# A fused attention and gated MLP kernel: where the MLP output's row pairs, its last gates and its last two token tiles stand

## The chip, the core and the metric

The kernel runs on one core of one Trainium2 chip. The core has five engines that run side by side and meet through semaphores: TensorE (PE, matmuls, with its weight loads shown as PEld), VectorE (DVE), ScalarE (ACT), GpSimd (POOL) and SyncE (SP, which here issues the DMAs). The metric is the device time of one launch in microseconds, the median of a few runs. Lower is better.

## The reference

The input x has shape (2, 2048, 256). It is layer-normalised to xn, and two branches read xn: a global attention s with 16 heads, and a two-layer local network, whose SiLU gates s. Cut to what matters here:

```python
xn = layernorm(x)
s = attn_ref(xn)                   # 16 heads of 16, spatial bias, projection, + layernorm(xn)
h = xn
for l in range(2):                 # DEPTH
    h = h + local_attention(shift(h)) @ wo[l]          # 8 heads of 64, windows of 128
    a, g = split(layer_norm(shift(h)) @ w1[l] + b1[l]) # 682 columns each
    h = h + (a * gelu(g)) @ w2[l] + b2[l]
return x + s * silu(h)
```

All numbers are float32. shift moves the second half of the features by one token.

## The kernel before

The program first runs the global attention (to about 1690 us) and writes s to DRAM. The local network, `ffn_branch`, takes the rest. It works on **slots**: slot s is one layer, one batch and one chunk of 512 tokens, 16 slots in all, in the order layer, chunk, batch. Slots 0 to 7 belong to layer 0, 8 to 15 to layer 1. Each slot has four token tiles of 128. The loop (from `for n in range(len(tiles) + 4)`) runs one **step** per tile, n = 4 s + i, with i from 0 to 3, plus four steps after the last tile. The order of the work is written out by hand: `STEP` lists the operations of a step, and nothing is reordered later.

- T0, T1 (`a_turn`, L969): transposes of q and k of the tile before. Each is a set of matmuls that use half of the array's rows, in pairs for the rows 0 to 63 and 64 to 127. W0, W1 (`a_weights`, L1057) are half-row transposes as well, S0, S1 (`a_scores`, L997) use quarters, A0, A1 (`a_sums`, L1077) half of the columns. Everything else on PE uses the full array.
- R hands out the pieces of the layer norm's root (`f_var_at`), Q, K, V (`a_project`, L924) project the tile.
- F runs what is in `xs`: at i = 1 the attention's output for slot s-1 (`a_out`, L1092), at i = 2 and 3 the MLP's output for slot s-3, half k = 0 and 1 (`f_out`), and at i = 3 the mean for slot s-1 (`f_mean`, L1115).
- the three G take pieces from `gq`, the MLP's gates of slot s-2. A gate m has a matmul for its Gelu half (n = 1, then ScalarE, L1179) and one for its linear half (n = 0, then VectorE writes u, L1183). Per step i = 0, 1, 2, 3 they take 5, 2, 2 and 3 pieces.

The 682 hidden columns are five full blocks of 128 and a sixth of 42. `f_last` (L1195) computes the sixth with both halves in one matmul; VectorE writes `u_last` on 42 partitions (L1199) and POOL copies it to the partitions 64 and up (L1202). `u_last` is one buffer for all slots. In `f_out` the sixth block is a **row pair** (`both_halves`, L1214): two matmuls with 64 rows each, one in each half of the array, into two PSUM banks. float32 makes two passes of each, so the profile counts four.

In layer 0 `f_out` has 20 matmul passes into two banks `py`, the pair, and then two VectorE adds into the running state (`residual`, L902). The last token's column is held back in `held` until `f_mean` of the next chunk has read it. In layer 1 a half k is two token tiles: for each, ten passes into `pz` and two transposes of the state into `pzx` (L1242, L1248); then the pair, VectorE's `y = pzx + b2` (L1255) and two adds of `pz` (L1257). A closure `gate` is put into `gates`: SiLU on ScalarE, two POOL operations with s and x (L1261, L1262), and the store by SP. Gates run at the end of the step that made them. s and x of a half are loaded at the start of its first part, into one buffer each.

PSUM has eight banks, and `bank` hands them out in turn: a new tile waits for those that read the tile eight calls earlier. A DMA of `nc.sync` waits in SP's queue, in order.

After the loop, slots 14 and 15 are finished by hand: gates and outputs in turn, then all gates that are left.

Of the kernel before, what the change touches and what calls it, by code (L numbers as in the profile page):

```python
# [12 lines left out]
AF = mybir.ActivationFunctionType  # L13
ALU = mybir.AluOpType
# [3 lines left out]
B, N, D = 2, 2048, 256  # L18
P = 128
NT = N // P  # L20
CH = 512
NCH = N // CH
# [13 lines left out]
NM = (HID + P - 1) // P  # L36
MASKED = -1e30
HALVES = [slice(r * HD2, (r + 1) * HD2) for r in range(2)]
# [782 lines left out]
def ffn_branch(  # L821
# [9 lines left out]
    nc = tc.nc  # L831
    with ExitStack() as ctx:
# [3 lines left out]
        W, load_scales, load_tables, load_qkv, load_o, load_1, load_2 = weights  # L836
# [3 lines left out]
        h, mw = P // 2, HID - (NM - 1) * P  # L840
# [3 lines left out]
        u_last = cp.tile([P, CH], F32, name="u_last")  # L844
# [15 lines left out]
        def bank(name, shape=(P, CH)):  # L860
            turn[0] += 1
            return psr.tile(list(shape), F32, tag=BANKS[turn[0] % 8], name=name)
# [16 lines left out]
        def all_due():  # L879
            while later:  # L880
                later.pop(0)[1]()
# [6 lines left out]

        held = {}

        def residual(kind, b, cc, k, ps, col, part=slice(0, CH)):


            at = 1 + cc * CH + part.start
            w = part.stop - part.start
            n = w if k == 0 or cc == NCH - 1 or part.stop < CH else w - 1
            x = xA[b][:, k, at : at + w]
            if n < w:
                h = pool.tile([P, 1], F32, tag=f"held{kind}{b}", name=f"held{kind}_{b}_{cc}")
                nc.vector.scalar_tensor_tensor(h, ps[:, n:w], col, x[:, n:], ALU.add, ALU.add)  # L900
                held[kind, b] = (cc, h)
            nc.vector.scalar_tensor_tensor(x[:, :n], ps[:, :n], col, x[:, :n], ALU.add, ALU.add)  # L902

        def release(kind, b):
            if (kind, b) in held:
                cc, h = held.pop((kind, b))
                at = (cc + 1) * CH
                nc.vector.tensor_copy(xA[b][:, 1, at : at + 1], h)
# [202 lines left out]
        def f_mean(s):  # L1111
            l, b, cc = slots[s]
            hs = halves(s)
            pm = bank(f"pm_{s}")
            nc.tensor.matmul(pm, mean_w, fs[s]["hc"][:, 0, :], start=True, stop=True)  # L1115
            hc = fs[s]["hc"]
            for k in range(2):
                nc.vector.tensor_sub(hc[:, k, :], hs[k], pm)
            release("f", b)
            sq = pool.tile([P, 2, CH], F32, tag="sq", name=f"sq_{s}", bufs=1)  # L1120
            fs[s] = {"hc": hc, "sq": sq, "u": {}}
            soon(1, lambda: nc.scalar.activation(sq, hc, AF.Square))
            soon(2, lambda: nc.gpsimd.tensor_add(sq[:, 0, :], sq[:, 0, :], sq[:, 1, :]))
# [37 lines left out]
        def f_gate(s, m, n):  # L1161

            l, b, cc = slots[s]
            nm = f"{s}_{m}_{n}"
            V = vecs[:, l, :]
            mw = min(P, HID - m * P)
            at = n * HID + m * P
            if mw < P:
                return f_last(s, m, mw)
            hc = fs[s]["hc"]  # L1170
            assert fs[s].get("ready")
            ps = bank(f"pg_{nm}")
            for k in range(2):
                nc.tensor.matmul(  # L1174
                    ps[:mw], W["1"][:, k, at : at + mw], hc[:, k, :], start=(k == 0), stop=(k == 1)
                )
            if n == 1:
                gl = next_gl(nm)
                nc.scalar.activation(gl[:mw], ps[:mw], AF.Gelu, bias=V[:mw, NM + m : NM + m + 1])  # L1179
                fs[s]["gl"] = gl  # L1180
            else:
                u = pool.tile([P, CH], F32, tag="u", name=f"u_{nm}", bufs=8)
                nc.vector.scalar_tensor_tensor(  # L1183
                    u[:mw], ps[:mw], V[:mw, m : m + 1], fs[s]["gl"][:mw], ALU.add, ALU.mult
                )
                fs[s]["u"][m] = u

        def f_last(s, m, mw):
# [12 lines left out]
            )  # L1201
            soon(1, lambda: nc.gpsimd.tensor_copy(u_last[h : h + mw], u_last[:mw]))  # L1202

        def f_out(s, k, part):

            l, b, cc = slots[s]
            F = fs[s]
            V = vecs[:, l, :]
            full = NM - 1

            def both_halves(to, lhs, rhs):

                for q, rows in enumerate(HALVES):
                    nc.tensor.matmul(to[q], lhs(q)[rows], rhs(q)[rows], start=False, stop=True)  # L1214

            if l < DEPTH - 1:
                cols = [slice(q * CH // 2, (q + 1) * CH // 2) for q in range(2)]
                w2 = W["2"][:, :, k * P : (k + 1) * P]
                if part == 0:
                    F["py"] = [bank(f"py_{s}_{k}_{q}")[:, : CH // 2] for q in range(2)]  # L1220
                for q in range(2):
                    for m in range(3 * part, min(3 * part + 3, full)):
                        nc.tensor.matmul(
                            F["py"][q], w2[:, m, :], F["u"][m][:, cols[q]], start=(m == 0), stop=False
                        )
                if part == 1:
                    both_halves(F["py"], lambda q: w2[:, full, :], lambda q: u_last[:, cols[q]])
                    c0 = 2 * NM + 4 + k
                    for q in range(2):
                        residual("f", b, cc, k, F["py"][q], V[:, c0 : c0 + 1], cols[q])  # L1230
                return
            if part == 0:
                F["py"] = [bank(f"pz_{s}_{k}_{q}")[:, :D] for q in range(2)]
                F["xt"] = bank(f"pzx_{s}_{k}", (P, 2, D))
                F["s"] = shared(0, (P, 2, D), f"s_{s}_{k}")
                F["x"] = shared(1, (P, 2, D), f"x_{s}_{k}")
                F["y"] = shared(2 + k, (P, 2, D), f"y_{s}_{k}")
                nc.sync.dma_start(F["s"], s_out[b * NCH + cc][:, 2 * k : 2 * k + 2, :])
                nc.sync.dma_start(F["x"], x_ch[b * NCH + cc][:, 2 * k : 2 * k + 2, :])
            i = 2 * k + part  # L1240
            for m in range(full):
                nc.tensor.matmul(  # L1242
                    F["py"][part], F["u"][m][:, i * P : (i + 1) * P], W["2"][:, m, :], start=(m == 0),
                    stop=False,
                )
            for h in range(2):
                at = 1 + cc * CH + i * P
                nc.tensor.transpose(F["xt"][:, part, h * P : (h + 1) * P], xA[b][:, h, at : at + P], ident)  # L1248
            if part == 1:
                both_halves(  # L1250
                    F["py"], lambda q: u_last[:, (2 * k + q) * P : (2 * k + q + 1) * P],
                    lambda q: W["2"][:, full, :],
                )
                y, ys, yx = F["y"], F["s"], F["x"]
                nc.vector.tensor_add(y, F["xt"], b2_row[:, None, :].to_broadcast([P, 2, D]))  # L1255
                for q in range(2):
                    nc.vector.tensor_add(y[:, q, :], y[:, q, :], F["py"][q])  # L1257

                def gate():
                    nc.scalar.activation(y, y, AF.Silu)  # L1260
                    nc.gpsimd.tensor_mul(y, y, ys)  # L1261
                    nc.gpsimd.tensor_add(y, y, yx)  # L1262
                    nc.sync.dma_start(out_ch[b * NCH + cc][:, 2 * k : 2 * k + 2, :], y)

                gates.append(gate)


        gates = []
# [7 lines left out]
        def gate_pieces(s):  # L1276
            full = NM - 1
            ps = [(lambda m=m, n=n: f_gate(s, m, n)) for m in range(full) for n in (1, 0)]
            return ps[:4] + [lambda: f_gate(s, full, 1)] + ps[4:]

        clear(k_ring[0][:, :, P : 2 * P], *sms[:4])
        gq = []
# [1 line left out]
        for n in range(len(tiles) + 4):  # L1284
            s, i = divmod(n, TPC)
            cur, pre, pre2 = (tiles[x] if 0 <= x < len(tiles) else None for x in (n, n - 1, n - 2))
            order = START_STEPS[n] if n < 2 else FIRST_STEP if n <= N_FIRST else STEP

            def have(x):
# [35 lines left out]
            def run(q, n=1):  # L1325
                for _ in range(n):
                    if q:
                        piece(q.pop(0))
# [48 lines left out]
                load_o(1)  # L1377
            if s == per_layer + 2 and i == 0:
                load_1(1)
            if s == per_layer + 2 and i == 3:  # L1380
                load_2(1)
        s = n_slots + 1
        run(gq, 99)
        for k in range(2):
# [7 lines left out]
            g()  # L1392
        gates.clear()
        run(gq, 99)
        for k in range(2):
            run(out_pieces(s - 2, k), 2)
        all_due()
        for g in gates:
            g()
        gates.clear()  # L1400


# [87 lines left out]
```

## Time and profile before

| what | value |
|---|---|
| median of 3 runs | 3005.99 us (3005.26 to 3006.25) |
| the profiled execution's own time | 3006.25 us |
| its span, first to last instruction | 3004.5 us |
| mean granted TensorE clock | 0.995 |
| the stretch 1880 to 2500 us: PE, DVE, ACT, POOL busy | 620.0, 407.2, 374.7, 396.2 us |
| the stretch 2500 to 2910 us: PE, DVE, ACT, POOL busy | 410.0, 268.7, 266.8, 274.9 us |
| last store issued | 3001.15 us |

The span is what the hardware profiler sees from the first instruction to the last; the time of the same execution is a little longer. Busy times come from the stretches view. A timeline line gives the start in us, the length in us, the engine, the source line, the operation, its tiles (out<-in), shapes and the number of merged instructions; in brackets the idle time before it and what ended that. Lengths of matmuls are modelled and overlap the next one, so on PE the distance between starts is what counts. A waits view lists which engine waited for which, in total, how often and the longest.

### The profile page before, as it was taken

How to read it: one execution, taken by the hardware profiler on the slowest of the kernel's cores; microseconds unless marked ns; L12 is line 12 of the kernel's file. 1: busy time of each engine (PE TensorE's matmuls, PEld its weight loads, DVE VectorE, ACT ScalarE, POOL GpSimd, SP SyncE). 2: the span in 40 equal slices, each digit the busy share in tenths (PEclk: the TensorE clock that was granted, in tenths of full speed). 3: DMA queues.
4: the chain of work that ended last, by engine and by line, in shares of the span. 5: the costliest groups of instructions: out<-in, count | busy, mean ns of one | idle time of the engine just before them, and what ended most of it. 6: DMA issues, size and time to landing. Idle time of an engine off the chain costs nothing. (4 is left out here: it accounts for less than half of the span.)

```text
span 3004.5 us, 60909 instructions
## 1 busy us (share of the span) xinstructions
PE 2964.5 (99%) x22764; PEld 1368.1 (46%) x22764; DVE 2211.6 (74%) x4840; ACT 2125.3 (71%) x4528; POOL 1618.2 (54%) x1463
## 2 busy tenths in 40 slices
PE   8999999999999999999999999999999999999998
PEld 3433333333333333333333465555555555565565
DVE  6898888788887788888885576666666666666653
ACT  4788877788887788888888655656666556666653
POOL 3575434446544354353444565666666666667642
PEclk9999999999999999999999999999999999999999
DMA  3100100000001100010000200000000000000001
GB/s 122 31 8 17 35 18 25 30 15 21 23 16 53 53 8 25 13 26 9 8 9 25 76 10 1 8 1 8 1 5 33 1 21 18 22 22 22 22 22 56
DMA packets 65963, 70.77 MB, mean 24 GB/s; under 512 B 28772, under 2 KB 44300, under 8 KB 65668
## 3 DMA queue, kind: packets, MB, share of 16 engines
q1 hardware_dynamic: 64770, 66.09, 7.3%
q8 instruction: 180, 2.95, 0.4%
q14 instruction: 115, 0.94, 0.1%
q10 hardware_dynamic: 386, 0.52, 0.1%
q0 software_dynamic: 512, 0.26, 0.0%
HBM read 45.35 MB, written 17.53 MB: 21 GB/s over the span
## 5 line engine op out<-in xcount | busy, mean ns | idle before, releaser
L439 DVE TENSOR_REDUCE mx<-pm 128x1 f32<-128x512 f32 x2048 | 1270.4, 683 | 218.3 <-PE ps L480 207.6
L482 ACT ACTIVATE e<-ps 128x512 f32<-128x512 f32 x2048 | 1058.3, 603 | 246.9 <-PE ps L480 245.6
L436 PE MATMUL pm<-kT,qT 32*128 32x512 f32 x4096 | 1020.1, 617 | 5.3 <-DVE mx L439 5.1
L480 PE MATMUL ps<-qa,kT 32*128 32x512 f32 x4096 | 1013.5, 616 | 0.0
L513 POOL TENSOR_TENSOR o<-o,part 128x512 f32<-128x512 f32 x465 | 590.0, 1269 | 776.5 <-ACT part L512 771.5
L436 PEld LDWEIGHTS pm<-kT,qT 32*128 32x128 f32 x4096 | 403.0, 184 | 409.9 <-DVE mx L439 385.2
L498 PE MATMUL po<-e,v 128*32 128x512 f32 x4096 | 546.6, 606 | 0.0
L480 PEld LDWEIGHTS ps<-qa,kT 32*128 32x128 f32 x4096 | 398.1, 184 | 187.2 <-ACT e L482 107.3
L1036 POOL TENSOR_TENSOR sm<-sm,wls 128x384 f32<-128x384 f32 x224 | 180.4, 826 | 339.5 <-DVE wls L1025 332.5
L924 PE MATMUL pp<-weights,xA 128*128 128x512 f32 x768 | 348.9, 601 | 0.0
L512 ACT COPY part<-po 128x512 f32<-128x512 f32 x465 | 287.0, 617 | 6.7 <-PE po L498 5.5
L1174 PE MATMUL pg<-hc,weights 128*128 128x512 f32 x640 | 286.2, 595 | 0.0
L498 PEld LDWEIGHTS po<-e,v 128*32 128x32 f32 x4096 | 81.0, 108 | 389.3 <-ACT e L482 359.7
L1019 ACT ACTIVATE sm<-sm,wmx 128x192 f32<-128x192 f32 x512 | 225.3, 441 | 8.9 <-DVE wmx L1011 8.2
L955 POOL TENSOR_TENSOR rn<-rn,mhalf 128x8 f32<-128x8 f32 x128 | 215.6, 1684 | 9.8 <-DVE rn L954 5.2
L924 PEld LDWEIGHTS pp<-weights,xA 128*128 128x128 f32 x768 | 141.6, 190 | 165.7 <-issue 164.4
L945 ACT ACTIVATE sqq<-pp 128x512 f32<-128x512 f32 x128 | 76.4, 597 | 173.9 <-DVE swp L943 157.6
L1174 PEld LDWEIGHTS pg<-hc,weights 128*128 128x128 f32 x640 | 120.5, 190 | 150.9 <-issue 143.3
L946 POOL TENSOR_TENSOR rot<-rot,swp 128x512 f32<-128x512 f32 x128 | 163.8, 1293 | 34.0 <-DVE swp L943 30.4
L1179 ACT ACTIVATE gl<-pg,vecs 128x512 f32<-128x512 f32 x80 | 54.6, 683 | 148.3 <-PE pg L1174 148.0
L1183 DVE SCALAR_TENSOR_TENSOR u<-pg,vecs,gl 128x512 f32<-128x512 f32 x80 | 59.8, 747 | 132.0 <-PE pg L1174 132.0
L1011 DVE CUSTOM_DVE_ANT_0 sm<-ps,mask 128x192 f32<-128x192 f32 x512 | 147.0, 354 | 4.7 <-PE ps L997 4.3
(183 smaller groups left out, 3415.3 us busy)
## 6 DMA issues: line engine op xcount, KB each, us to landing
s<-in_x_dram SPq DMA_DIRECT2D x8, 512.0 KB
qk_wk<-stage_wk SPq DMA_DIRECT2D x16, 256.0 KB
kT<-qk_wk SPq DMA_DIRECT2D x128, 32.0 KB
qk_wq<-stage_wq SPq DMA_DIRECT2D x16, 256.0 KB
qT<-qk_wq SPq DMA_DIRECT2D x128, 32.0 KB
qa<-qk_wq SPq DMA_DIRECT2D x128, 32.0 KB
s_out<-s SPq DMA_DIRECT2D x8, 512.0 KB
s<-s_out SPq DMA_DIRECT2D x16, 256.0 KB
```

Source lines behind the costliest of these rows:

```text
L436: nc.tensor.matmul(ps, qT[rows, q0 : q0 + P], kT[rows, c * CH : (c + 1) * CH], start=True, stop=True)
L439: nc.vector.tensor_reduce(mxs[n][:, j * TPC + i, c : c + 1], ps, AX.X, ALU.max)
L480: nc.tensor.matmul(ps, kT[rows, kt * P : (kt + 1) * P], qas[n % 2][rows, :], start=True, stop=True)
L482: nc.scalar.activation(e, ps, AF.Exp)
L498: nc.tensor.matmul(po[j * HP : (j + 1) * HP, :], v[:, kt, (r + j) * VW : (r + j) * VW + HP], es.pop((n, kt, j)), start=True, stop=True,)
L512: nc.scalar.copy(part, po)
L513: nc.gpsimd.tensor_add(os[n], os[n], part)
L924: nc.tensor.matmul(ps, xA[b][:, k, at : at + P], W["qkv"][:, k, n * INNER : (n + 1) * INNER], start=(k == 0), stop=(k == 1),)
L955: nc.gpsimd.tensor_tensor(rn, rn, mhalf, ALU.pow)
L1019: nc.scalar.activation(sm[:, x, IN], sm[:, x, IN], AF.Exp, scale=-1.0, bias=mx[:, hb, r, x : x + 1], accum_out=ls[:, hb, r, x : x + 1],)
L1036: nc.gpsimd.tensor_mul(sm, sm, ls[:, hb, r, :, None].to_broadcast([P, 2, WIN]))
L1174: nc.tensor.matmul(ps[:mw], W["1"][:, k, at : at + mw], hc[:, k, :], start=(k == 0), stop=(k == 1))
```

## The change

- In `f_out`, the pair and what reads it become a closure. For slots 0 to 12 it goes into `pairs`, and `close_pairs` runs it at the start of the next step, in front of that step's T0. For later slots it runs at once.
- Layer 0's adds (`rest`) stand behind the pair. Since they now come after `f_mean`, nothing is held back, and `release("f", b)` goes.
- In layer 1, `rest` also loads s and x (`load_sx`), and the gate it makes runs at the end of the step in which the pair stands.
- `f_last` moves from the fifth place of a slot's gate pieces to the ninth. So the step i = 3 ends with the Gelu half of gate 3, and `f_last` is in i = 0.
- Layer 1's w2 is loaded behind the first `close_pairs` of the next step.
- The last slot's half k = 1 is done tile by tile: transposes first, b2 added at once, the sixth block as one half-row matmul; SiLU on ScalarE, product and sum with s and x on VectorE, and a store for each tile. Its s and x have buffers of their own, loaded in its first part. The gate of k = 0 runs ahead of it.

The diff's core:

```diff
-            release("f", b)
+        pairs = []
+        def row_pair(s, to, lhs, rhs, then):
+            def f():
+                for q, rows in enumerate(HALVES):
+                    nc.tensor.matmul(to[q], lhs[q][rows], rhs[q][rows], start=False, stop=True)
+                then()
+            if s + 3 < n_slots:
+                pairs.append(f)
+            else:
+                f()
+        def close_pairs():
+            while pairs:
+                pairs.pop(0)()
+        def load_sx(s, k, tag):
...
+            for i, src in enumerate((s_out, x_ch)):
+                x = shared(tag + i, (P, 2, D), f"{'sx'[i]}_{s}_{k}")
+                nc.sync.dma_start(x, src[b * NCH + cc][:, 2 * k : 2 * k + 2, :])
...
+                def rest():
...
+                    for q in range(2):
+                        nc.vector.scalar_tensor_tensor(
+                            x[:, cols[q]], py[q], V[:, c0 : c0 + 1], x[:, cols[q]], ALU.add, ALU.add
                         )
                 if part == 1:
-                    both_halves(F["py"], lambda q: w2[:, full, :], lambda q: u_last[:, cols[q]])
...
+                    row_pair(s, py, [w2[:, full, :]] * 2, [u_last[:, c] for c in cols], rest)
                 return
+            last = s == n_slots - 1 and k == 1
             if part == 0:
...
-                nc.sync.dma_start(F["s"], s_out[b * NCH + cc][:, 2 * k : 2 * k + 2, :])
-                nc.sync.dma_start(F["x"], x_ch[b * NCH + cc][:, 2 * k : 2 * k + 2, :])
+                if last:
+                    F["sx"] = load_sx(s, k, 4)
...
+            if last:
+                turn_x()
+                nc.vector.tensor_add(y[:, part, :], xt[:, part, :], b2_row)
+            for m in range(full + last):
+                rows = HALVES[0] if m == full else slice(0, P)
+                u = (u_last if m == full else F["u"][m])[rows, i * P : (i + 1) * P]
+                nc.tensor.matmul(py[part], u, W["2"][rows, m, :], start=(m == 0), stop=last and m == full)
+            if last:
+                yp = y[:, part, :]
+                nc.vector.tensor_add(yp, yp, py[part])
+                nc.scalar.activation(yp, yp, AF.Silu)
+                nc.vector.tensor_mul(yp, yp, F["sx"][0][:, part, :])
+                nc.vector.tensor_add(yp, yp, F["sx"][1][:, part, :])
+                nc.sync.dma_start(out_ch[b * NCH + cc][:, i, :], yp)
+                return
+            turn_x()
+            def rest():
+                ys, yx = load_sx(s, k, 0)
+                nc.vector.tensor_add(y, xt, b2_row[:, None, :].to_broadcast([P, 2, D]))
...
+            if part == 1:
+                lhs = [u_last[:, (2 * k + q) * P : (2 * k + q + 1) * P] for q in range(2)]
+                row_pair(s, py, lhs, [W["2"][:, full, :]] * 2, rest)
...
-            return ps[:4] + [lambda: f_gate(s, full, 1)] + ps[4:]
+            return ps[:8] + [lambda: f_gate(s, full, 1)] + ps[8:]
...
+            close_pairs()
+            if s == per_layer + 3 and i == 0:
+                load_2(1)
...
-            if s == per_layer + 2 and i == 3:
-                load_2(1)
...
+        all_due()
         for k in range(2):
             run(out_pieces(s - 2, k), 2)
-        all_due()
-        for g in gates:
-            g()
-        gates.clear()
+            for g in gates:
+                g()
+            gates.clear()
```

More of the change, by code (lines that the diff above doesn't have):

```diff
@@ L889, in ffn_branch, with residual @@
         held = {}
[L891 to L898, printed above, removed]
+        def residual(kind, b, cc, k, ps, col):
+            at = 1 + cc * CH
+            n = CH if k == 0 or cc == NCH - 1 else CH - 1
+            x = xA[b][:, k, at : at + CH]
+            if n < CH:
                 h = pool.tile([P, 1], F32, tag=f"held{kind}{b}", name=f"held{kind}_{b}_{cc}")
-                nc.vector.scalar_tensor_tensor(h, ps[:, n:w], col, x[:, n:], ALU.add, ALU.add)
+                nc.vector.scalar_tensor_tensor(h, ps[:, n:], col, x[:, n:], ALU.add, ALU.add)
                 held[kind, b] = (cc, h)
@@ L1202, in f_last @@
             soon(1, lambda: nc.gpsimd.tensor_copy(u_last[h : h + mw], u_last[:mw]))
+        pairs = []
[12 more added lines that the diff above has]
+        def load_sx(s, k, tag):
+            l, b, cc = slots[s]
+            both = []
+            for i, src in enumerate((s_out, x_ch)):
+                x = shared(tag + i, (P, 2, D), f"{'sx'[i]}_{s}_{k}")
+                nc.sync.dma_start(x, src[b * NCH + cc][:, 2 * k : 2 * k + 2, :])
+                both.append(x)
+            return both
         def f_out(s, k, part):
@@ L1209, in f_out @@
             full = NM - 1
-            def both_halves(to, lhs, rhs):
-                for q, rows in enumerate(HALVES):
-                    nc.tensor.matmul(to[q], lhs(q)[rows], rhs(q)[rows], start=False, stop=True)
             if l < DEPTH - 1:
@@ L1220, in f_out @@
                     F["py"] = [bank(f"py_{s}_{k}_{q}")[:, : CH // 2] for q in range(2)]
+                py = F["py"]
                 for q in range(2):
                     for m in range(3 * part, min(3 * part + 3, full)):
-                        nc.tensor.matmul(
-                            F["py"][q], w2[:, m, :], F["u"][m][:, cols[q]], start=(m == 0), stop=False
+                        nc.tensor.matmul(py[q], w2[:, m, :], F["u"][m][:, cols[q]], start=(m == 0), stop=False)
+                def rest():
+                    c0 = 2 * NM + 4 + k
+                    x = xA[b][:, k, 1 + cc * CH : 1 + (cc + 1) * CH]
+                    for q in range(2):
+                        nc.vector.scalar_tensor_tensor(
+                            x[:, cols[q]], py[q], V[:, c0 : c0 + 1], x[:, cols[q]], ALU.add, ALU.add
                         )
                 if part == 1:
-                    both_halves(F["py"], lambda q: w2[:, full, :], lambda q: u_last[:, cols[q]])
-                    c0 = 2 * NM + 4 + k
-                    for q in range(2):
-                        residual("f", b, cc, k, F["py"][q], V[:, c0 : c0 + 1], cols[q])
+                    row_pair(s, py, [w2[:, full, :]] * 2, [u_last[:, c] for c in cols], rest)
                 return
+            last = s == n_slots - 1 and k == 1
             if part == 0:
@@ L1234, in f_out @@
                 F["xt"] = bank(f"pzx_{s}_{k}", (P, 2, D))
-                F["s"] = shared(0, (P, 2, D), f"s_{s}_{k}")
-                F["x"] = shared(1, (P, 2, D), f"x_{s}_{k}")
                 F["y"] = shared(2 + k, (P, 2, D), f"y_{s}_{k}")
-                nc.sync.dma_start(F["s"], s_out[b * NCH + cc][:, 2 * k : 2 * k + 2, :])
-                nc.sync.dma_start(F["x"], x_ch[b * NCH + cc][:, 2 * k : 2 * k + 2, :])
+                if last:
+                    F["sx"] = load_sx(s, k, 4)
             i = 2 * k + part
[L1241 to L1245, printed above, removed]
@@ L1246, in f_out @@
-            for h in range(2):
-                at = 1 + cc * CH + i * P
[L1248 to L1255, printed above, removed]
+            py, xt, y = F["py"], F["xt"], F["y"]
@@ new lines, in turn_x @@
+            def turn_x():
+                at = 1 + cc * CH + i * P
+                for h in range(2):
+                    nc.tensor.transpose(xt[:, part, h * P : (h + 1) * P], xA[b][:, h, at : at + P], ident)
+            if last:
[5 more added lines that the diff above has]
+                nc.tensor.matmul(py[part], u, W["2"][rows, m, :], start=(m == 0), stop=last and m == full)
@@ L1256, in f_out @@
                 for q in range(2):
-                    nc.vector.tensor_add(y[:, q, :], y[:, q, :], F["py"][q])
+                    nc.vector.tensor_add(y[:, q, :], y[:, q, :], py[q])
                 def gate():
```

## The prediction, made before the changed kernel was run

> **What bounds the kernel now.** I read the page first, then who waited for whom on PE, then the timeline of PE around one step's end, then VectorE's over the same microseconds, and last all engines in the tail.
>
> ```profile
> PE 2964.5 (99%) x22764; PEld 1368.1 (46%) x22764; DVE 2211.6 (74%) x4840; ACT 2125.3 (71%) x4528; POOL 1618.2 (54%) x1463
> ```
>
> PE is busy 99% of the span, and the list of waits on PE between 1900 and 2900 us has no line at all: from the first moved pair to the last, PE never waits and only streams. So time taken from PE's stream there is time gained, and any new wait of PE is time lost, one for one. PE's timeline (start, length, engine, line, operation) over a boundary of two steps in layer 0:
>
> ```profile
> 2398.19 0.71 PE L969 MATMUL pt<-ident,rot 64*128 64x64 f32 x16
> 2398.74 1.16 PE L1057 MATMUL pw<-ident,sm 64*128 64x64 f32 x32
> 2399.83 1.53 PE L997 MATMUL ps<-k_ring,xT 64*64 64x192 f32 x32
> ...
> 2408.45 4.48 PE L1223 MATMUL py<-u,w 128*128 128x256 f32 x20
> 2412.86 0.70 PE L1214 MATMUL py<-u_last,w 64*128 64x256 f32 x4
> 2413.49 1.13 PE L1115 MATMUL pm<-hc,mean_w 128*128 128x512 f32 x2
> 2414.45 1.88 PE L1195 MATMUL pg<-hc,weights 128*128 128x512 f32 x4
> ```
>
> The pair (L1214) stands between full-array matmuls and takes 2413.49 - 2412.86 = 0.63. Two other places show the same neighbours without the change of shape: a pair directly before half-row transposes, and pm (L1115) after a full-array matmul.
>
> ```profile
> 2917.51 0.70 PE L1214 MATMUL pz<-w,u_last 64*128 64x256 f32 x4
> 2918.04 1.16 PE L1057 MATMUL pw<-ident,sm 64*128 64x64 f32 x32
> ```
>
> ```profile
> 2938.30 1.02 PE L1115 MATMUL pm<-hc,mean_w 128*128 128x512 f32 x2
> 2939.16 3.60 PE L1174 MATMUL pg<-hc,weights 128*128 128x512 f32 x8
> ```
>
> **Part 1: what the move saves.** Before half-row transposes the pair takes 0.53 instead of 0.63. pm takes 0.86 instead of the 0.96 behind a pair: 0.10. The 20 py take 4.41 to the pair; the tail's ten L1242 take 2.16 (2993.52 to 2995.68), so 20 are 4.32 and entry costs 0.09. T0 and T1 (L969) take 0.55 from a full-array predecessor; half of L1057's 32 inside the mode, (1.09 - 0.09)/2, are 0.50: 0.05. T0's own entry is paid either way. Together 0.10 + 0.10 + 0.09 + 0.05 = **0.34 a pair**. Moved are slots 0 to 12, two pairs each: 26 x 0.34 = **8.8 us** off.
>
> **Part 2: the wait that takes its place.** Before, the pair's banks were read by VectorE under the gates' matmuls. Now the pair stands last, and the eight banks come round. Counting `bank` calls from the pair's first bank: in layer 0 after i=2 (py, py, two gates, T0 two, T1 two) W0 gets the pair's banks; after i=3 (py, py, pm, three gates, T0 two) T1 gets them. In layer 1 pzx takes one more: after i=2 T1's second and W0's first bank, after i=3 T0's second and T1's first. The built program has just these waits on VectorE's adds. VectorE at this boundary:
>
> ```profile
> 2394.66 0.88 DVE L902 SCALAR_TENSOR_TENSOR xA<-py,vecs,xA 128x256 f32<-128x256 f32 x2 [1.31 <-PE py L1214]
> ...
> 2398.37 0.75 DVE L1183 SCALAR_TENSOR_TENSOR u<-pg,vecs,gl 128x512 f32<-128x512 f32 x1 [2.83 <-PE pg L1174]
> 2399.04 0.75 DVE L978 COPY k_ring<-pt 128x256 f32<-128x256 f32 x2
> 2399.70 1.28 DVE L1060 COPY pT<-pw 128x512 f32<-128x512 f32 x2
> ```
>
> Set t=0 where T0 starts before (2398.19). The pair will start there, T0 at 0.53, T1 at 0.78, W0 at 1.03 if nothing waits. VectorE's first add can start 0.73 after the pair (2394.66 - 2393.93; the pair before it in the same timeline), and two take 0.88; PE follows VectorE by some 0.05 (k_ring's copies end at 2399.79, S0's matmuls start at 2399.83).
> - Layer 0, after i=2: the last gate's u (L1183) holds VectorE until 2399.04, t=0.85. Adds end at 1.73, W0's second bank comes at 1.78 instead of 1.03: **0.75**.
> - Layer 0, after i=3: the step now ends with a ScalarE gate, VectorE is free, adds run 0.73 to 1.61, T1's second bank comes at 1.66 instead of 0.78: **0.88**.
> - Layer 1, after i=2: b2's add (0.69) and two y adds, in the tail 2996.15 to 2997.70 = 1.55 (first y add done at 1.22), start at 0.85. T1 waits to 2.12, ends at 2.37, W0 waits for the second add, 2.40, to 2.45 instead of 1.03: **1.42**.
> - Layer 1, after i=3: b2's add needs no pair and is done early; the y adds run 0.73 to 1.48. T0's second bank comes at 1.20, T1's at 1.53, W0 at 1.78: 0.75. Then S0 (1.09 behind W0, 2.87) wants xT, and ScalarE has Gelu, Silu's table, Silu and the copies in a row:
>
> ```profile
> 2577.33 0.69 ACT L1179 ACTIVATE gl<-pg,vecs 128x512 f32<-128x512 f32 x1
> 2578.03 1.28 ACT L1260 ACT_TABLE_LOAD   x1
> 2579.32 0.63 ACT L1260 ACTIVATE y<-y 128x512 f32<-128x512 f32 x1
> 2579.86 0.63 ACT L973 COPY xT<-pt 128x256 f32<-128x256 f32 x2
> ```
>
> That is 3.16 from Gelu's start to both copies. Before, a second matmul gate (1.72) covered it; now Gelu is last and starts at about t=0.1 (0.20 behind its gate's matmuls, less T0's entry), so S0 waits to 3.32: 0.45 more, **1.20**.
>
> Stalls: 8 x (0.75 + 0.88) + 5 x (1.42 + 1.20) = 13.0 + 13.1 = **26.1**. Against 8.8 saved: **+17.3**. Bounds: by the nearest row of a pair without waiting, 0 (then -8.8 remains); above, 26 x 1.55 = 40 if the layer 1 chain were uncovered everywhere. I take the worked values, since each bank and its releaser is in the program and each length is a row.
>
> The Trainium skill has a rule on each side, on one page (TensorEngine Tiling): section Key Properties says that a change of tiling mode drains TensorE, section PSUM Bottleneck that tiling leaves PSUM evacuation as slow as it was. The 0.10 behind a pair is the first, the 0.88 of VectorE's adds the second; by the first alone the time would be 2997, by both it is the sum below.
>
> **Part 3: the smaller moves.** `u_last`'s STT (0.74) goes from i=3 into i=0, ahead of the fourth reciprocal, where VectorE idles 0.36 before the last u (2437.94): the k_ring copies there come some 0.1 to 0.25 later, and S0 (0.04 behind them at 2399.83) has nothing to spare. I take 0.1 in 14 steps: **+1.4** (0 to 3.5). In the first step after the last tile (2913.5) PE already waits 0.4 for a u that now stands behind `u_last`: **+0.6** (0 to 0.7). Costed at nothing: s and x loads and the gate a step later, on SP, ScalarE and POOL (PE's 18 to 21 us step covers them; transfers take 3.1, and SP's stores only queue behind that POOL work); the dropped `held` copies (VectorE idle 1.31 to 2.35 there); w2's load (two steps before use; the uncovered price would be one transfer). The i=3 to i=0 gate of ScalarE is counted above.
>
> **Part 4: the tail.** The last instructions before:
>
> ```profile
> 2995.58 1.27 POOL L1262 TENSOR_TENSOR y<-y,x 128x512 f32<-128x512 f32 x1
> ...
> 2996.15 0.69 DVE L1255 TENSOR_TENSOR y<-pzx,b_row 128x512 f32<-128x512 f32 x1 [4.04 <-POOL y L1261]
> 2996.88 0.37 SPq L1239 DMA_DIRECT2D x<-in_x_dram  x1
> 2996.95 0.75 DVE L1257 TENSOR_TENSOR y<-y,pz 128x256 f32<-128x256 f32 x2
> 2997.30 4.22 SPq L1263 DMA_DIRECT2D out_dram<-y  x2
> ...
> 2999.86 1.26 POOL L1262 TENSOR_TENSOR y<-y,x 128x512 f32<-128x512 f32 x1
> ```
>
> The last store is issued at 3001.15. Single tiles gated by VectorE would cut the chain, but `load_sx` for k=1 now comes in SP's order behind the store of k=0, which waits for POOL until 2996.85. So s and x are issued at about 2997.5 and 2997.9; issue to use took 3.1 for such an x (2977.42 to POOL's 2980.55), so the first tile's last add runs at 3001.0. Behind it on VectorE stands all of the second tile: that add, b2, py, product and sum at 0.42 each (a 256-wide L1257), Silu about 0.40 (between the 0.37 of a 256-wide copy and 0.63 for 512), gaps 0.3: 2.8, store at 3003.8: **+2.7**. With the loads early it would be -1.8: py of the last tile ends 0.8 later (its half-row matmul no longer shares a pass), then 0.42 + 0.40 + 2 x 0.42 and gaps put the store at 2999.4. I take +2.7 and keep both ends.
> The skill (DMA: Bandwidth & Descriptors, section Anatomy of one DMA) gives a fixed 2.0 us and 436 GB/s, by estimate 2.6 for 256 KB: the tail would be +2.2.
>
> **Sum.** 17.3 + 1.4 + 0.6 + 2.7 = +22.0. The profiled execution took 3006.25 (its span 3004.5 and 1.75 around it), 0.26 above the median 3005.99; from the median: **3028.0**.
>
> **Rivals.**
> - The switches alone (faster): at every moved pair VectorE's adds end before PE comes to the pair's banks, so only the 0.34 is felt: 3006.0 - 8.8 + 2.7 = 2999.9, or 2995.4 with early loads in the tail. For it, the switches are plain in PE's rows; against it, the adds' 0.88. It decides where 0.73 and the adds together stay under the 1.03 to W0 (layer 0, i=2), 0.30 for the two adds. 0.08.
> - The change half does what it says: the stalls are half covered, because T0 and T1 run on while VectorE ends: -8.8 + 13.0 + 4.7 = +8.9, 3015 and down to 3009 with the tail early. For it, VectorE's 0.85 at t=0 is one row's; against it, all boundaries of before look alike. 0.08, half of it counted within 0.2%.
> - Later engines do not catch up (exps and k_ring late as well, another 0.4 a boundary): 3036 to 3042. For it, VectorE runs without a gap from u through the sm rows; against it, the stall gives VectorE time. 0.05.
> - My sum: 0.79, of its own 3017 to 3036.
>
> **How the numbers follow.** 0.2% is 6 us, about what can be told from no change here. Faster by more: 0.08; within (3000 to 3012): 0.04; slower: 0.88. The range 3011 to 3037 holds the own range and part of two rivals, some 0.84, and the bounds of the tail (-4.5) and u_last (+2).
>
> **What would show it.** In the profile after: L1208's pairs right before L968 at 0.53; waits of PE pt and pw on DVE xA and y, 26 places, together near 25 us; pm back at 0.86; S0's wait on ACT xT five times; s and x of the last tiles issued after the store of k=0. Wrong if PE has no wait on those adds, or if its waits there stay under 10 us in all.

## The result, and the profile after

The changed kernel takes **3030.71 us** (median of 5 runs, 3029.75 to 3033.99); the kernel before, run beside it, 3006.02. The ratio is 1.0079 (95% interval 1.0069 to 1.0090): slower by 24.7. The forecast was 3028.0 in 3011 to 3037. The profiled span grew from 3004.5 to 3029.0.

The page's line of busy times:

```profile
PE 2971.3 (98%) x22764; PEld 1378.3 (46%) x22764; DVE 2208.2 (73%) x4833; ACT 2126.0 (70%) x4530; POOL 1615.4 (53%) x1461
```

PE has the same 22764 matmuls, and its share fell from 99% to 98%. Between 1880 and 2920 us the kernel before has one line of PE's waits, of 0.4 us, behind the last tile (told further down). Now there are three (who waits, for what; us in all, times, longest):

```profile
PE pt L968 <- DVE y L1292: 7.9, 10, 1.1
PE pt L968 <- DVE xA L1249: 3.4, 8, 0.4
PE pw L1056 <- DVE xA L1249: 1.5, 8, 0.2
```

The 26 places that the prediction named are there: 8 + 8 in layer 0, 10 in layer 1. Their 12.8 us are half of the "near 25" that it gave as a sign, and not far above the 10 that would have shown it wrong. They are only part of the loss, since idle time is counted from the modelled ends of matmuls; the distances between starts are the measure. Of the other signs, pm takes 0.86 again (2582.15 to 2583.01). S0's wait for xT is in the list of the weight loads, and not only after i = 3, as foreseen, but as often after i = 0 (here for two slots, from 2690 to 2850 us):

```profile
PEld ps L996 <- ACT xT L972: 0.8, 4, 0.3
```

The boundary in layer 0 after i = 2, PE first, then VectorE:

```profile
2404.39 0.70 PE L1208 MATMUL py<-u_last,w 64*128 64x256 f32 x4
2404.93 0.67 PE L968 MATMUL pt<-ident,rot 64*128 64x64 f32 x16
2405.78 1.60 PE L1056 MATMUL pw<-ident,sm 64*128 64x64 f32 x32 [0.18 <-DVE xA L1249]
2407.30 1.53 PE L996 MATMUL ps<-k_ring,xT 64*64 64x192 f32 x32
```

```profile
2404.58 0.75 DVE L1181 SCALAR_TENSOR_TENSOR u<-pg,vecs,gl 128x512 f32<-128x512 f32 x1 [4.18 <-PE pg L1172]
2405.24 0.87 DVE L1249 SCALAR_TENSOR_TENSOR xA<-py,vecs,xA 128x256 f32<-128x256 f32 x2
```

The pair takes 2404.93 - 2404.39 = 0.54 in its new place. T (L968) runs 0.85 to W, W (L1056) 1.52 to S instead of 1.09: it waits for the adds L1249, which stand behind the last u and end at 2406.11.

The boundary in layer 1 after i = 3, PE and ScalarE:

```profile
2588.25 0.70 PE L1208 MATMUL pz<-w,u_last 64*128 64x256 f32 x4
2588.42 0.69 ACT L1177 ACTIVATE gl<-pg,vecs 128x512 f32<-128x512 f32 x1 [1.86 <-PE pg L1172]
...
2589.12 1.28 ACT L1295 ACT_TABLE_LOAD   x1
...
2589.46 0.88 PE L968 MATMUL pt<-ident,rot 64*128 64x64 f32 x15 [0.46 <-DVE y L1292]
...
2590.96 0.63 ACT L972 COPY xT<-pt 128x256 f32<-128x256 f32 x2
...
2591.36 1.80 PE L996 MATMUL ps<-k_ring,xT 64*64 64x192 f32 x32
...
2593.09 0.66 PE L1076 MATMUL po<-pT,v 128*64 128x128 f32 x8
```

Here T waits for the y adds, and S0 starts on the first of the two xT copies; the second ends at 2591.59.

From here on, E is the end of the last gate's streaming: 0.43 (the distance between two such matmuls) after the start of its last matmul. Before, T0 starts at E + 0.09, S0 at E + 1.73. Behind a pair, S0 is due at E + 2.21, if nothing waits (that is where it stands in the one kind of such boundary without a wait, told below), and A0 1.46 later, at 3.67. The length of a slot is the distance from A0 to A0 four steps on.

| stretch | before | after | difference | forecast |
|---|---|---|---|---|
| a slot of layer 0 (8 with pairs) | 79.14 | 80.18 | +1.04 (one +1.26), together 8.5 | 8.4 |
| a slot of layer 1 (5) | 80.06 | 82.50 (the first 82.06) | +2.44 x 4 and +2.0, together 11.8 | 10.2 |
| A0 in the first step after the last tile, to slot 15's first pz | 83.31 | 84.44 | +1.1 | +0.6 |
| slot 15's first pz to the span's end | 18.91 | 21.46 | +2.55 | +2.7 |

That is 24.0 of the 24.5 us between the spans; the forecast's column adds up to 21.9. The other 0.6 stand already ahead of the first moved pair and are not the change's: in the traces below, the local network starts between 1.4 us earlier and 3.4 us later than in that of the kernel before. So lengths of slots tell small effects better than medians.

### The profile page after: what moved, and what is told of

It is laid out like the page before. It is cut to its first block, busy times and chain, and to the rows that moved or that the text cites. A ratio compares the mean times of both kernels' runs of the same rounds, so it can differ in the third digit from the quotient of the medians.

```text
span 3029.0 us, 60896 instructions
## 1 busy us (share of the span) xinstructions
PE 2971.3 (98%) x22764; PEld 1378.3 (46%) x22764; DVE 2208.2 (73%) x4833; ACT 2126.0 (70%) x4530; POOL 1615.4 (53%) x1461
## 4 chain that ended last, share of the span: by engine, by line
PE 92%; DVE 3%; ACT 2%; POOL 1%; DMA 1%; issue 1%; SPq 0%; POOLq 0%; ACTq 0%; DVEq 0%
PE pm L436 18%; PE po L498 17%; PE ps L480 15%; PE pp L923 10%; PE pg L1172 8%; PE px L1091 4%; PE po L1076 4%; PE ps L996 3%; PE py L1243 2%; PE pz L1277 2%; PE pw L1056 2%; PE px L610 1%; PE pp_wk L364 1%; PE pp_wq L364 1%; PE pv L402 1%; PE pt L968 1%
```

## Experiments

Theory: PE waits for the pair's two banks behind VectorE's adds, in layer 1 for ScalarE's xT too, and the tail waits for late loads. Rivals: VectorE would be late without the banks; u_last's move or the loads make the loss; the tail's chain is bound elsewhere. A median stands beside the kernel before on the same chip (3007.5, 3007.0 and 3006.7 in the three sets); the finer readings are from the traces. The expectations place S0 at E + 2.27, 0.06 too late, since they left out the 0.05 that T saves behind a pair.

**The tail's loads early.**

```diff
                 ys, yx = load_sx(s, k, 0)
+                if s == n_slots - 1:
+                    F["sx"] = load_sx(s, 1, 4)
...
-                if last:
-                    F["sx"] = load_sx(s, k, 4)
```

> Only the tail differs from the changed kernel (3030.7): s and x of the last two tiles are issued right behind those of the half before, so they are there when the product wants them. Theory (the wait for s and x is the whole loss of the tail): the last tile's matmuls end at 3019.4 as before, then y add, Silu, product, sum of 0.42 each with gaps of about 0.1, last store at 3021.6 instead of 3026.2: -4.6, so 3026.1, and from slot 15's first pz to the span's end 16.9 instead of 21.5. Rival (the tail's chain is bound by VectorE's order or by PE, the loads are covered): no change, 3030.7. Rival (the loads wait for the buffer that gl held or share the queues): between, 3028.

3025.1; the tail takes 16.71 instead of 21.46. The last tiles of the changed kernel, all engines:

```profile
3018.86 0.38 SPq L1298 DMA_DIRECT2D out_dram<-y  x1
3019.55 0.33 SPq L1225 DMA_DIRECT2D s<-s_out  x1
...
3022.80 0.43 DVE L1282 TENSOR_TENSOR y<-y,s 128x256 f32<-128x256 f32 x1 [6.09 <-DMA s<-s_out]
```

and of this kernel:

```profile
3017.41 0.70 PE L1275 MATMUL pz<-w,u_last 64*128 64x256 f32 x2
...
3018.33 0.42 DVE L1278 TENSOR_TENSOR y<-y,pz 128x256 f32<-128x256 f32 x1
```

In the first, s and x are issued behind the store of k = 0, and the product runs 3.25 after s was issued, with VectorE idle for 6.09. In the second the last tile's y add follows its matmuls (0.92 after the half-row matmul starts), and Silu, product and sum follow at once. The wait for s and x was the tail's whole loss; with them early, the new tail ends 18.91 - 16.71 = 2.2 sooner than the old.

**All pairs at once**, where the kernel before has them (with `held` again); u_last's place and the tail as changed.

```diff
-            if s + 3 < n_slots:
+            if False:
                 pairs.append(f)
```

> The changed kernel with every pair run where the kernel before ran it; the place of u_last's gate, of the b2 weights' load and the tail stay as changed. Theory (all of the loss but the tail's comes from the pairs' banks and from the gates that follow the pairs): 3006.0 + 2.5 for the tail + 0 to 1.4 for u_last = 3008.5 to 3010. Rival (u_last's move makes the 0.45 that layer 1 loses after i=0, five times): 3010.8 to 3011, and S0 after i=0 in layer 1 still at E+1.92. Rival (the loss is not with the pairs): above 3020.

3019.6 (ratio 1.0041, 1.0026 to 1.0056): too slow for the theory, and neither rival's number, if only just (the last one's began at 3020). Layer 0 takes 79.15 a slot, as before. Layer 1 takes 81.78, 1.72 over before, and S0 after i = 0 is on time (E + 1.74), so the second expectation fell as well. PE's waits have one line, and the boundary after i = 3 shows it, ScalarE first, then PE:

```profile
PE ps L997 <- ACT xT L973: 7.0, 5, 1.4
```

```profile
2578.81 0.69 ACT L1179 ACTIVATE gl<-pg,vecs 128x512 f32<-128x512 f32 x1 [1.86 <-PE pg L1174]
2579.52 1.28 ACT L1294 ACT_TABLE_LOAD   x1
...
2581.35 0.63 ACT L973 COPY xT<-pt 128x256 f32<-128x256 f32 x2
```

```profile
2579.19 1.16 PE L1057 MATMUL pw<-ident,sm 64*128 64x64 f32 x32
2581.75 1.80 PE L997 MATMUL ps<-k_ring,xT 64*64 64x192 f32 x32 [1.40 <-ACT xT L973]
```

With u_last's gate gone to i = 0, the step i = 3 ends with a Gelu instead of a gate of VectorE, and Silu and xT queue up behind it. S0 starts at E + 3.20 and A0 at 4.93, exactly as in the changed kernel, though no pair stands there. At this boundary the moved pair adds nothing to the wait; the later of two waits decides.

**Banks skipped behind the pairs of layer 0.** The list gives how many banks each following call of `bank` skips, by layer and step.

```diff
+        SKIPS = {(0, 3): [0, 0, 0, 0, 2], (0, 0): [0, 0, 2]}
...
-            turn[0] += 1
+            turn[0] += 1 + (skips.pop(0) if skips else 0)
...
+                skips[:] = SKIPS.get((l, i), [])
```

> In layer 0 two banks are skipped behind each moved pair, so that nobody wants the pair's two banks before S0 or S1; VectorE's order stays. In the changed kernel S0 stands 0.74 (after i=2) and 0.88 (after i=3) late in those 16 boundaries, 13.0 us. Theory with both steps (banks first, and behind them k_ring's copies, which stand behind the adds on VectorE): W0 no longer waits, but S0 waits for k_ring: adds from 0.94 and 0.82 after E, 0.88, copies 0.74, PE 0.04: S0 at 2.60 and 2.48 instead of 2.27, stalls 0.34 and 0.21, gain 8 x (0.40 + 0.67) = 8.5, time 3022.2. Rival (the banks are all of it): gain 13.0, time 3017.7. Rival (the banks are not what PE waits for, VectorE is late anyway): 3030.7 and S0 as late as now.

3020.4; a slot of layer 0 takes 78.97. PE has no wait on VectorE's adds there any more (W starts at E + 1.12). What is left has the foreseen size: A0 stands 0.32 (after i = 2) and 0.20 (after i = 3) late, for 0.34 and 0.21. The reason is only in part the foreseen one. The boundary after i = 2, ScalarE, PE and VectorE:

```profile
2397.00 0.65 ACT L975 COPY xT<-pt 128x256 f32<-128x256 f32 x2 [1.90 <-PE pt L971]
...
2397.07 1.34 PE L1059 MATMUL pw<-ident,sm 64*128 64x64 f32 x32
2397.66 0.74 DVE L980 COPY k_ring<-pt 128x256 f32<-128x256 f32 x2
...
2398.34 1.65 PE L999 MATMUL ps<-k_ring,xT 64*64 64x192 f32 x32
```

W takes 1.27 to S0 instead of 1.09: the skip gave W1 the banks of T0, which ScalarE's xT copies free (they end at 2397.65). So S0 starts at E + 2.41, 0.20 late, at both boundaries. Only the other 0.12 after i = 2 are k_ring's, whose second copy ends at 2398.40 and which the second part of S0 waits for. The banks do come first; behind them comes mainly xT, which the expectation did not name. That the sizes agree is luck.

**The same, and one k_ring copy on ScalarE at these boundaries** (`closed[0]` is the layer of the pairs that the step began with).

```diff
-                nc.vector.tensor_copy(k_ring[b][:, :, at : at + HD2], pss[r])
+                on_act = r == 0 and closed[0] == 0
+                (nc.scalar.copy if on_act else nc.vector.tensor_copy)(k_ring[b][:, :, at : at + HD2], pss[r])
```

> As the kernel with the banks skipped in layer 0, and at those boundaries one of k_ring's two copies goes to ScalarE (0.37 us less on VectorE). Theory (banks, then VectorE's order): VectorE's adds and one copy end at E+2.19, S0 is due at 2.27, so no stall is left in layer 0 and the gain against the changed kernel is 13.0: 3017.7. If k_ring were not what is late next, it would be the same as the kernel without this edit, 3022; if A0's pT is late in its turn, between, 3019 to 3021, with S0 on time and A0 over 3.73 after E.

3018.75, and a slot takes 78.85; S0 stands at 2.41 and A0 at 3.87 after i = 2 and after i = 3 alike, both 0.20 late. So k_ring's 0.12 are gone, and the wait for xT is left, which none of the three cases names. ScalarE, then PE:

```profile
2397.30 0.65 ACT L975 COPY xT<-pt 128x256 f32<-128x256 f32 x2 [1.90 <-PE pt L971]
```

```profile
2397.37 1.34 PE L1060 MATMUL pw<-ident,sm 64*128 64x64 f32 x32
2398.64 0.56 PE L1000 MATMUL ps<-k_ring,xT 64*64 64x192 f32 x8
```

xT ends at 2397.95, W takes 1.27 to S instead of 1.09. The skip moved part of the wait from VectorE's adds to ScalarE's copies.

**b2's add of layer 1 ahead of the pair.**

```diff
             def rest():
                 ys, yx = load_sx(s, k, 0)
-                nc.vector.tensor_add(y, xt, b2_row[:, None, :].to_broadcast([P, 2, D]))
...
             if part == 1:
+                nc.vector.tensor_add(y, xt, b2_row[:, None, :].to_broadcast([P, 2, D]))
                 lhs = [u_last[:, (2 * k + q) * P : (2 * k + q + 1) * P] for q in range(2)]
```

> The changed kernel (3030.7) with b2's add of layer 1 issued right behind the transposes, not behind the pair. Theory (after i=2 in layer 1 T1 and W0 wait for VectorE's three adds in a row, b2's 0.69 first): without it the y adds run from E+0.94 to 1.69, W0 starts at 1.74 to 1.79 instead of 2.54, S0 at 2.83 to 2.88 instead of 3.68: 0.8 x 5 = 4.0 less. After i=3 nothing changes, since S0 there waits for ScalarE's xT (A0 stays at 4.93). Time 3026.7. Rival (ScalarE's xT also bounds S0 after i=2): no change, S0 stays near 3.7. Rival (the banks' wait after i=3 counts as well): 3024 or less.

3026.6, as expected; a slot takes 81.71. S0 after i = 2 is at 2.89 instead of 3.68, and A0 after i = 3 still at 4.93. Of PE's waits the line for y goes from 7.9 to half:

```profile
PE pt L968 <- DVE y L1291: 3.9, 10, 0.5
```

**Gates where Gelu's table is loaded.**

```diff
+                    if i % 2:
+                        for g in gates:
+                            g()
+                        gates.clear()
                     if gq:
                         nc.scalar.activation(gelu_table, eps_t, AF.Gelu)
...
-            for g in gates:
-                g()
-            gates.clear()
+            if s == n_slots:
+                for g in gates:
+                    g()
+                gates.clear()
```

> The changed kernel with the gates of y (Silu, product, sum, store) put ahead of the Gelu table's load in steps i=3 and i=1 instead of at the end of steps 3 and 0. Theory (in layer 1 S0 after i=3 and after i=0 waits for ScalarE, which has Gelu, Silu's table, Silu and xT in a row): after i=0 S0 goes from E+1.92 to 1.73 and A0 from 5.34 to 4.89, 0.45; after i=3 the banks' wait is left, S0 at 3.1, A0 at 4.55 instead of 4.93, 0.38. Together 0.83 x 5 = 4.1 less, 3026.6. Rival (the wait is for VectorE alone): no change. Rival (a Silu ahead of the Gelu gates makes u late): PE waits in front of py or px instead, 3030 or more.

3026.9; a slot takes 81.70. After i = 0, S0 is back at 1.74; on ScalarE no Silu stands between Gelu and xT there:

```profile
2605.97 0.69 ACT L1177 ACTIVATE gl<-pg,vecs 128x512 f32<-128x512 f32 x1 [0.60 <-DVE u L1181]
2607.58 0.65 ACT L972 COPY xT<-pt 128x256 f32<-128x256 f32 x2 [0.92 <-PE pt L968]
```

After i = 3, S0 is at 3.11 and A0 at 4.57: with ScalarE out of the way, the banks alone hold A0 back by 0.90.

**The old gate order, pairs at once, the tail with early loads.**

> Pairs at once and u_last's gate in its old place (after the second u), the tail with single tiles and early loads. In the kernel with the pairs at once but the gate moved, layer 1 took 81.78 a slot against 80.06, all of it after i=3, where S0 waited for xT. Theory (moving u_last's gate makes a Gelu the last gate at i=3, and with Silu's table behind it xT comes late): 80.06 a slot again, tail -2.1, so 3003.9. Rival (it comes from the other edits of the gates and loads, w2's load or the order in f_out): still 81.78, 3012.5.

3004.64 (ratio 0.9992, 0.9984 to 1.0001). Its edit is `ps[:4]` for `ps[:8]` on top of the two edits above. Layer 1 takes 80.06 again, and the stretch from the first step after the last tile to slot 15's first pz 83.38, not 84.44. So the order of the gates makes both losses.

**Banks skipped in layer 1 alone**, with b2's add early and the gates left at the steps' ends: the same list with `(1, 3): [0, 0, 0, 2], (1, 0): [0, 2]`.

> The kernel with b2's add early (3026.6; 81.71 a slot in layer 1), and two banks skipped behind each moved pair of layer 1; the gates stay at the ends of the steps. Theory (after i=3 in layer 1 two waits lie beside each other, VectorE's adds for the banks and ScalarE's Gelu, Silu table and Silu for xT, and the later one decides): after i=2 S0 goes from E+2.89 to about 2.45, after i=3 S0 stays at 3.20 and A0 at 4.93 although T0, T1 and W0 no longer wait for banks: 81.27 a slot, 5 x 0.44 = 2.2 less, 3024.4. Rival (the two waits add up): S0 after i=3 comes at 2.5, another 0.7 a slot less, 80.6, 3021.

3025.9, and 81.61 a slot, where the theory had 81.27 and the rival 80.6: neither. After i = 2 S0 is at 2.41, as expected. After i = 3 A0 comes at 5.31, later than the 4.93 without the edit. ScalarE's xT and PE there:

```profile
2752.46 0.63 ACT L975 COPY xT<-pt 128x256 f32<-128x256 f32 x2
...
2752.86 0.71 PE L1059 MATMUL pw<-ident,sm 64*128 64x64 f32 x16 [1.42 <-ACT xT L975]
```

W1 got T0's bank again, and now half of W, not only S0, stands behind xT. That ScalarE decides this boundary holds; that the two waits merely lie beside each other was too simple, as the skip moved one wait onto the other.

**All edits together** (banks in both layers, one k_ring copy on ScalarE, b2's add early, gates at the table, early loads).

> All edits together: banks skipped in both layers, one k_ring copy on ScalarE at those boundaries, b2's add early, gates at the Gelu table's place, s and x of the last tiles early. Layer 0 as measured alone, 78.85 a slot against 79.14 before. Layer 1 by the same reckoning: 0.68 saved by the switches, twice 0.19 left to W1's wait for the bank that xT frees: 79.76 against 80.06. Against the kernel before: 8 x -0.29, 5 x -0.30, first step behind the last tile +1.1, tail -2.1: -4.8, so 3001.2, within 0.2% of before and under it. If other waits turn up in layer 1 behind these, 3003 to 3008.

**3000.35** (10 runs), ratio 0.9977 (0.9968 to 0.9986): faster than both kernels. Layer 0 takes 78.85, layer 1 79.53. The boundary after i = 3 in layer 1 has no wait:

```profile
2733.94 0.70 PE L1212 MATMUL pz<-w,u_last 64*128 64x256 f32 x4
...
2736.05 0.72 PE L1000 MATMUL ps<-k_ring,xT 64*64 64x192 f32 x12
```

S0 starts 2.11 behind the pair, at E + 2.21 (pair 0.53, T 0.49, W 1.09): this is the due time used above. Against the kernel before, 8 x 0.29 + 5 x 0.53 and the tail's 2.2 are won and 1.1 is lost behind the last tile: 6.1, and the medians differ by 6.7. The old gate order together with moved pairs would need a second buffer for u_last; it was not tried.

## Why the prediction was right, and where it was off

**Part 1 (the switches save 0.34 a pair) held.** Where the waits are known, the slot's length follows from it. With the bank skips and the copy on ScalarE, layer 0 should be 79.14 - 2 x 0.34 + 2 x 0.20 = 78.86; it is 78.85. With all edits, layer 1 should be 80.06 - 0.68 + 0.20 (after i = 2 alone) = 79.58; it is 79.53. The gain was there, and it was paid back at the same boundaries.

**Part 2 (the banks) held in layer 0 and after i = 2 in layer 1.** S0 is late by 0.80 and 0.93 for the forecast 0.75 and 0.88, and by 1.47 for 1.42. By the starts the 26 stalls are 27.5 us, for 26.1. The bank skips took the wait away in layer 0, and the early b2 add took its own part in layer 1. Part of what the stalls have over the forecast stands in W: after i = 3 in layer 0 and after i = 2 in layer 1 it takes 1.14 to S0 behind the wait, not 1.09; why is not shown.

**Part 2 after i = 3 in layer 1: right in size, 1.26 for 1.20, with one thing unseen.** The prediction had S0 wait for xT as the last link of the pair's price ("0.45 more"). Without any pair that wait is 1.74. So it belongs to the gate order, not to the pair. The prediction's lower bound, 0 for all stalls, and its rival of the switches alone could not have come about with these gates: with no wait for banks at all, A0 would still come at 4.93 there, as it does with the pairs at once: 5 x 1.26 = 6.3 of the 8.8.

The row that sets this wait is ScalarE's table load: 1.28, with Silu 1.30 behind its start. The Trainium skill (ScalarE: Activation LUTs, section What ACT_TABLE_LOAD costs) adds a drain to it and gives 2.66 for a switch; no such gap stands in the rows after i = 0 below (2607.64 to 2608.94), and the measurement decides.

**Part 3 failed in two places.** VectorE's write of u_last was to cost 0.1 in 14 steps, by delaying k_ring after i = 0. Layer 0 with the move alone takes 79.15 for 79.14: nothing. And the step that was "Costed at nothing: s and x loads and the gate a step later" cost 0.45 four times in layer 1, 1.8 us: the gate of k = 1 now ends step 0, where its Silu table and Silu stand between the last Gelu and xT. (The gate of the fifth such half, slot 12's, falls behind the last tile, where no scores follow.)

```profile
2606.94 0.69 ACT L1177 ACTIVATE gl<-pg,vecs 128x512 f32<-128x512 f32 x1 [0.59 <-DVE u L1181]
2607.64 1.28 ACT L1295 ACT_TABLE_LOAD   x1
2608.94 0.63 ACT L1295 ACTIVATE y<-y 128x512 f32<-128x512 f32 x1
2609.48 0.63 ACT L972 COPY xT<-pt 128x256 f32<-128x256 f32 x2
```

E is 2607.97 here; xT ends at 2610.11, and S0's first half starts at 2609.88. The prediction weighed the cover by the length of the step, 18 to 21 us; what counts is the 2.1 us from the end of the last Gelu (2607.63) to the time S0 is due (2609.70), and table load, Silu and xT take 2.5. With the gates at the table's place the wait was gone. The stretch behind the last tile was +0.6 and is +1.1. PE's waits there, in the changed kernel and then in the one before:

```profile
PE pz L1277 <- DVE u L1181: 1.2, 2, 1.0
```

```profile
PE pz L1242 <- DVE u L1183: 0.4, 1, 0.4
```

The old gate order takes that back.

**Part 4 held from both ends**: +2.55 for +2.7 with late loads, -2.2 for -1.8 with early ones. The +2.2 by the figures of the Trainium skill (DMA: Bandwidth & Descriptors, section Anatomy of one DMA) is further off: the page gives them for DMAs issued by GpSimd, and here SP issues them; s took 3.25 from issue to use, not the estimated 2.6.

Of the rivals, the switches alone and the half-covered stalls are ruled out by the 26 waits and their sizes; "later engines do not catch up" has a grain of truth: in layer 1 another 0.45 in four slots, but on ScalarE and for a reason of its own. The forecast's total was 2.7 too low: 1.8 is the gate after i = 0, 0.5 the stretch behind the last tile, and 0.6 stood ahead of the first pair; the tail was 0.15 under its term. The 0.05 to 0.06 by which each of the 26 stalls was longer, together 1.4, makes up for the 1.4 that u_last was given; that these two errors cancel is luck.

## What to carry to other kernels

An accumulation that is closed late holds its banks late: count the allocations from its first bank to the next user, and put its reader's place in that engine's queue beside the time until then. When work moves across a step, look at what stands last on every engine at the new boundary; a step of 20 us hides nothing of a table load that falls into its last 2 us. Two waits at one boundary are told apart only by taking away each alone and both, and moving a bank off one reader can put it on another. A forecast that is met in size can still have the wrong engine: name the row that must go, and take it away.

## What was not expected of the hardware

In the tail with early loads, VectorE's 256-wide sum took 1.38 instead of 0.42, beside a POOL operation on other data:

```profile
3016.28 1.33 POOL L1297 TENSOR_TENSOR y<-y,x 128x512 f32<-128x512 f32 x1
3016.52 1.38 DVE L1281 TENSOR_TENSOR y<-y,x 128x256 f32<-128x256 f32 x1
```

It ended at 3017.90, 0.29 after POOL's end. The Trainium skill (SBUF — State Buffer, section SBUF: two separate sides) says that a VectorE operation with two SBUF inputs and a GpSimd operation that reads SBUF exclude each other: whichever starts first keeps the shared ports for its whole length, and the other waits. These rows agree: POOL starts first, and both inputs of the sum are in SBUF. An add with one input in PSUM, 1.5 us earlier, took its usual 0.42 in the midst of another POOL operation:

```profile
3014.93 1.28 POOL L1296 TENSOR_TENSOR y<-y,s 128x512 f32<-128x512 f32 x1 [9.65 <-ACT y L1295]
3014.99 0.42 DVE L1278 TENSOR_TENSOR y<-y,pz 128x256 f32<-128x256 f32 x1 [1.85 <-PE pz L1275]
```

The longer sum cost under 0.2 here, as the second tile's matmuls ran until 3018.11.
